# Prompts' keys as four more columns of each head's score product, in a two-branch cross-attention kernel

## The chip, the cores and the metric

The kernel runs on one core of a Trainium2 chip. Its time is the device time in microseconds of one execution, as the median of several runs. All data are 32-bit floats.

## What is computed

There are eight batches of 112 queries with 320 channels (20 heads of 16), and 375 context rows of 512 values each, of which the first 371 are text tokens and the last four are prompts. Cut to what matters, the reference is:

```python
q = heads(hidden_states @ W_q)
k_t, v_t = heads(text_ehs @ W_k), heads(text_ehs @ W_v)
probs_t = softmax(q @ k_t.T * attn_scale)
text_out = probs_t @ v_t
k_ip, v_ip = heads(ip_ehs @ W_k_ip), heads(ip_ehs @ W_v_ip)
attn_scores = q @ k_ip.T * attn_scale              # the prompts' logits: 112 x 4 a head
sem = l2norm(probs_t @ text_ehs) @ l2norm(ip_ehs).T
probs_ip = softmax(attn_scores + 0.5 * sem) * spatial_mask
out = (text_out + probs_ip @ v_ip) @ W_out + b_out + hidden_states
```

The change concerns how `attn_scores`, the prompts' logits, come about.

## The kernel before, in words

**Groups.** The 20 heads of a batch form five groups of four (`groups`, g = 0 to 4). A head takes 32 partitions of TensorE's rows, so the four heads of a group can run side by side. A loop runs over `steps`, all 35 pairs (batch b, group g) of the first seven batches; the last batch has a loop of its own with more work put on ACT and POOL.

**One step.** `multiplied(b, g)` (L618) makes twelve rounds of four products (L631, one for each head) of the transposed probabilities with a matrix of values and of context products, into four PSUM banks. In its rounds j = 0 and j = 6 stand the scores of the group two steps ahead (`LEAD`), heads 2 and 3 and then heads 0 and 1. `scores` (L575) is one product of 112 queries with 371 text keys (L584), out of `qm`, which holds the projected and scaled queries with the other head of a pair of heads masked out, and `kT`, the keys. `probabilities` (L593) follows: DVE takes the negated maximum (L597), ACT the Exp into `p` (L601), and SP starts a DMA of `p` to `xg` (L604). For the pair at j = 0 this follows at once; for the pair at j = 6 it comes after the step's copies of sums (`value_sums`, L644 on ACT). `transposed` (L608) is DVE's transposition of the next group's `xg` at j = 2 (L612), and `reduced` (L673) makes DVE's four sums over the products (L677), which free the four banks for the next step. `placed` (L549) lets POOL write the next group's values into `u` (L553).

**Between steps.** `between(b, g)` (L871) puts pieces of other work after each step: the next batch's context products (`gram`, L411), values (L480), keys (L447 and, for the last third, transpositions L438), the next queries (`project_queries`, L279), the transposed context (L353), and pieces of `finish` for the batch before (L693). At g = 3 of each batch up to the seventh stands `prompt_logits(b)` (L557), between two pieces of the keys, and for the last batch it stands in the last loop after g = 0.

**The prompts' logits.** `prompt_projections` (L241) projects all 32 prompts at once into `kip` (channels by prompts) and multiplies it with a mask of heads into `kipb`, which has for each prompt a column for every head of the third, zero outside the head's channels. `prompt_logits` then makes three products (L564) of the queries `qT` with those columns, into one bank, and ACT copies 112x80 logits into `ipl` (L571). For this alone `project_queries` copies each product of the queries to `qT` on ACT (L315), behind DVE's masked copies of the same bank to `qm` (L312). `finish` reads `ipl` at L746.

**Order and banks.** The orders of TensorE, SP, DVE and, after the start, ACT are those written in the code; POOL's is a scheduler's until the last loop. There are eight PSUM banks in three rotations: four `ps_qd` (products L631), two `ps_sc` (scores, and with `spare` some of ps_c, ps_x and ps_a), two `ps_mm` (all else, `bank`). A bank's next user waits for all who read its last content.

Of the kernel before, what the change touches and what calls it, by code (L numbers as in the profile page):

```python
# [14 lines left out]
NIP = 4  # L15
# [5 lines left out]
def kernel(  # L21
# [170 lines left out]

    ipT = const.tile([P, NE, N], F32, tag="ipT", name="ipT")
    ipnT = const.tile([P, NE, N], F32, tag="ipnT", name="ipnT")
    kipb = const.tile([P, NC, B, HC, NIP], F32, tag="kipb", name="kipb")
    vipd = dram.tile([N, C], F32, tag="vipd", name="vipd", bufs=1)

    vipx = dram.tile([2, H, NIP, C], F32, tag="vipx", name="vipx", bufs=1)
# [42 lines left out]
    def prompt_projections():  # L241

        spread(nc.gpsimd, wkip_sb)
        for i in range(NC):
            ps = bank(f"ps_kip{i}")
            for e in range(NE):
                nc.tensor.matmul(
                    ps[:, :N],
                    wkip_sb[:, e, i * P : (i + 1) * P],
                    ipT[:, e, :],  # L250
                    start=(e == 0),
                    stop=(e == NE - 1),
                )
            kip = work.tile([P, N], F32, tag="kip", name=f"kip_{i}")
            nc.scalar.copy(kip, ps[:, :N])
            nc.vector.tensor_tensor(
                kipb[:, i],
                kip.rearrange("p (b n) -> p b n", n=NIP).unsqueeze(2).to_broadcast([P, B, HC, NIP]),
                hmask.unsqueeze(1).unsqueeze(3).to_broadcast([P, B, HC, NIP]),
                ALU.mult,  # L260
            )
            yield
        ps = bank("ps_vip")
        for e in range(NE):
            nc.tensor.matmul(
                ps[:N, :C], ipT[:, e, :], wvip_sb[:, e, :], start=(e == 0), stop=(e == NE - 1)
            )
        vip = work.tile([N, C], F32, tag="vip", name="vip", bufs=1)
        nc.scalar.copy(vip, ps[:N, :C])
        yield  # L270

        nc.sync.dma_start(vipd, vip)
        yield
# [5 lines left out]
    def project_queries(bs):  # L279
        n = len(bs)  # L280
        xT = work.tile([P, NC, 2 * S], F32, tag="xT", name=f"xT_{bs[0]}", bufs=1)
        qT = work.tile([P, NC, 2 * S], F32, tag="qT", name=f"qT_{bs[0]}", bufs=2)
        qm = work.tile([P, NC, 2, 2 * S], F32, tag="qm", name=f"qm_{bs[0]}", bufs=2)
        for j, b in enumerate(bs):
            queries[b] = (qT, qm, j)
        nc.gpsimd.memset(xT[REST:, FULL, :], 0.0)
        for i in range(NC):
            cn = min(P, C - i * P)
            if bs[0] == 0:

                ps = ps_qd.tile([P, 512], F32, tag="qd", name=f"ps_x_0_{i}")
            else:
                ps = bank(f"ps_x_{bs[0]}_{i}", spare=bs[0] > 1 and i > 0)
            for j, b in enumerate(bs):
                nc.tensor.transpose(
                    ps[:cn, j * S : (j + 1) * S], x_sb[:, b, i * P : i * P + cn], ident[:S, :S]
                )
            nc.scalar.copy(xT[:cn, i, : n * S], ps[:cn, : n * S])
            yield
        for i in range(NC):  # L300
            ps = bank(f"ps_q_{bs[0]}_{i}")
            for j in range(NC):
                nc.tensor.matmul(  # L303
                    ps[:, : n * S],
                    wq_sb[:, j, i * P : (i + 1) * P],
                    xT[:, j, : n * S],
                    start=(j == 0),
                    stop=(j == NC - 1),
                )

            for r in range(2 if i < FULL else 1):
                nc.vector.tensor_scalar_mul(  # L312
                    qm[:, i, r, : n * S], ps[:, : n * S], emask[:, r : r + 1]
                )
            nc.scalar.copy(qT[:, i, : n * S], ps[:, : n * S])  # L315
            yield


# [6 lines left out]
    def begin(b):  # L325
        s = st[b] = dict(ct=loaded.pop(b))
        s["ctxT"] = work.tile([P, NE, TP], F32, tag="ctxT", name=f"ctxT_{b}")
        nc.gpsimd.memset(s["ctxT"][:, :, T:], 0.0)
        s["kT"] = work.tile([P, NC, TT], F32, tag="kT", name=f"kT_{b}")
        s["vext"] = work.tile([P, NT, C + REST], F32, tag="vext", name=f"vext_{b}", bufs=1)  # L330
        s["k3"] = k3
        s["vd"] = dram.tile([TP, C], F32, tag="vd", name=f"vd_{b}")
        s["u"] = work.tile([P, UCOL], F32, tag="u", name=f"u_{b}")
        s["vr"] = work.tile([P, BLK, NG, D], F32, tag="vr", name=f"vr_{b}")
        s["ipl"] = work.tile([S, H, NIP], F32, tag="ipl", name=f"ipl_{b}")
        s["ss"] = work.tile([S, H], F32, tag="ss", name=f"ss_{b}")
        s["pvs"] = work.tile([S, H, VW], F32, tag="pvs", name=f"pvs_{b}")
        s["vip"] = work.tile([S, NIP, H, D], F32, tag="vipb", name=f"vip_{b}")
# [90 lines left out]

    def keys(b):  # L430
        s = st[b]
        for i in range(NC):
            ps = bank(f"ps_k_{b}_{i}")
            if 0 < b < B - 1 and i == FULL:

                for c in range(NT):
                    rows = min(P, TT - c * P)
                    nc.tensor.transpose(  # L438
                        ps[:, c * P : c * P + rows],
                        s["k3"][:rows, c].rearrange("p a r d -> p (a r d)"),  # L440
                        ident[:rows, :rows],
                    )
                nc.scalar.copy(s["kT"][:, i, :], ps[:, :TT])
                yield
                return
            for e in range(NE):
                nc.tensor.matmul(  # L447
                    ps[:, :TT],
                    wk_sb[:, e, i * P : (i + 1) * P],
                    s["ctxT"][:, e, :TT],  # L450
                    start=(e == 0),
                    stop=(e == NE - 1),
                )
            nc.scalar.copy(s["kT"][:, i, :], ps[:, :TT])  # L454
            yield

    def last_keys(b, ps):

        s = st[b]
        for e in range(NE):  # L460
            if e == NE // 2:
                yield
            nc.tensor.matmul(  # L463
                ps[:, :TT],
                wk_sb[:, e, FULL * P :],
                s["ctxT"][:, e, :TT],
                start=(e == 0),
                stop=(e == NE - 1),
            )
        nc.scalar.copy(s["kT"][:, FULL, :], ps[:, :TT])  # L470
        yield

    def values(b):
# [81 lines left out]
            )  # L555

    def prompt_logits(b):  # L557
        s = st[b]
        qT, _, j = queries[b]
        ps = bank(f"ps_ip_{b}")  # L560
        for i in range(NC):
            heads = slice(0, HC, 1) if i < FULL else slice(0, HC, 2)
            hn = min(HC, H - i * HC)
            nc.tensor.matmul(  # L564
                ps[:S, i * HC * NIP : (i * HC + hn) * NIP],
                qT[:, i, j * S : (j + 1) * S],
                kipb[:, i, b, heads, :],
                start=True,
                stop=True,
            )  # L570
        nc.scalar.copy(s["ipl"], ps[:S, :HN].rearrange("p (h n) -> p h n", n=NIP))  # L571
        yield


    def scores(b, g, a, early=False, ps=None):  # L575
        s = st[b]
        _, qm, j = queries[b]
        i, r = g // 2, g % 2
        if early and (g + a // 2) % 2:

            ps = ps_qd.tile([P, 512], F32, tag="qd", name=f"ps_s_{b}_{g}_{a}")
        elif ps is None:
            ps = ps_sc.tile([P, 512], F32, tag="sc", name=f"ps_s_{b}_{g}_{a}")
        nc.tensor.matmul(  # L584
            ps[:S, :TT],
            qm[a * RG : (a + 1) * RG, i, r, j * S : (j + 1) * S],
            s["kT"][a * RG : (a + 1) * RG, i, :],
            start=True,
            stop=True,
        )  # L590
        s["sc", g, a] = ps

    def probabilities(b, g, a):  # L593
# [5 lines left out]
            s["p", g] = work.tile([S, GROUP, TT], F32, tag="p", name=f"p_{b}_{g}", bufs=3)  # L599
        p = s["p", g][:, a, :]  # L600
        nc.scalar.activation(p, ps[:S, :TT], AF.Exp, bias=nmx)  # L601

        xg = x_ring[(b * NG + g) % NX]
        nc.sync.dma_start(  # L604
# [259 lines left out]
    def run(key, make, pieces=1):  # L864

        if key not in gens:
            gens[key] = make()
        for _ in range(pieces):
            next(gens[key], None)

    def between(b, g):  # L871
# [26 lines left out]
        if g == 3:  # L898
            if new:
                run(("k", nb), None, 1)  # L900
            for bs in first if b > 0 else ():
                run(("q", bs[0]), lambda: project_queries(bs), 3)
            run(("t", b), lambda: prompt_logits(b))
            if nb < B - 1:
                run(("k", nb), None, 1)
            if b > 0 and new:
# [131 lines left out]
    for g in range(NG):  # L1038
# [30 lines left out]
        if g == 0:  # L1069
            own_channels(bd)  # L1070
            with_bias(b)
            drain(prompt_logits(b))
            run(("f", b - 2), None)
        if g == 1:
            prompt_values(b)
# [77 lines left out]
```

## Time and profile before

| what | value |
|---|---|
| median of 3 runs (lowest, highest) | 450.31 us (450.1, 450.73) |
| the profiled execution: its own time | 450.23 us |
| its span, from the first to the last instruction | 448.5 us |
| mean granted TensorE clock | 0.998 |
| L584 scores, matmul records | 320, 470 ns median |
| L564 prompts' logits, matmul records | 48, 262 ns median |
| L601 Exp | 160, 570 ns median |
| L571 copies to `ipl` | 8, 226 ns median |
| L315 copies to `qT` | 15, 346 ns median |

A line of the profile names an engine (PE for TensorE's matmuls, PEld for its weight loads, DVE for VectorE, ACT for ScalarE, POOL for GpSimd, SP for the engine that issues the DMAs), the line of the kernel, the operation, and what it writes and reads. A 32-bit product shows as two records. Matmul records overlap: they begin when the product begins to stream, so that the distance between two starts is what one costs the stream.

### The profile page before, as it was taken

What the parts mean: (1) busy time and instruction counts of PE and PEld (TensorE: products, weight loads), DVE (VectorE), ACT (ScalarE), POOL (GpSimd) and SP (SyncE); (2) the same over time, 40 slices, a digit from 0 to 9 for tenths busy, and PEclk for the clock granted to TensorE, in tenths of its full rate; (3) what the DMA queues carried; (4) which work ended last, traced back from release to release, by engine and by line L of the source; (5) the groups of instructions that cost most, each with busy time, mean ns of one, the idle gap of its engine ahead of it and who ended that gap; (6) DMA issues with size and microseconds to landing.
All of it is one profiled execution on the core that took longest, in us unless ns stands there. A gap on an engine that the chain in (4) does not pass through costs nothing.

```text
span 448.5 us, 12974 instructions
## 1 busy us (share of the span) xinstructions
PE 435.1 (97%) x5137; PEld 336.2 (75%) x5137; DVE 308.2 (69%) x649; ACT 194.1 (43%) x543; POOL 110.0 (25%) x263
## 2 busy tenths in 40 slices
PE   8998999999999999999999999999999999999885
PEld 8756767887778777788777786788777887787682
DVE  4047366786687767686687866776687867878784
ACT  2254233345335353343434453343534353346782
POOL 4302200012050211511142120512123111527430
PEclk9999999999999999999999999999999999999999
DMA  8669964544645565545646366455656437453500
GB/s 243 183 164 252 203 143 140 141 142 143 169 122 130 144 172 163 137 118 142 163 127 158 113 177 162 126 136 143 163 163 144 134 88 190 127 141 103 144 2 26
DMA packets 52158, 64.83 MB, mean 145 GB/s; under 512 B 18370, under 2 KB 44146, under 8 KB 52098
## 3 DMA queue, kind: packets, MB, share of 16 engines
q1 hardware_dynamic: 51658, 63.45, 53.7%
q8 instruction: 40, 0.66, 0.7%
q10 hardware_dynamic: 440, 0.56, 0.4%
q14 instruction: 20, 0.16, 0.1%
HBM read 19.30 MB, written 5.32 MB: 55 GB/s over the span
## 4 chain that ended last, share of the span: by engine, by line
PE 88%; DVE 3%; ACT 3%; DMA 3%; issue 1%; POOL 1%; SPq 1%; DVEq 0%; ACTq 0%
PE ps_qd L631 41%; PE ps_v L480 14%; PE ps_k L447 9%; PE ps_g L411 8%; PE ps_s L584 4%; PE ps_q L303 3%; PE ps_c L353 2%; PE ps_o L848 2%; DMA xg<-p 1%; ACT p L601 1%; PE ps_g L383 1%; DVE junk L677 1%; PE ps_ip L564 1%; DVE xgT L612 1%; PE ps_k L463 1%
## 5 line engine op out<-in xcount | busy, mean ns | idle before, releaser
L631 PE MATMUL ps_qd<-u,xgT 32*112 32x104 f32 (+11 forms) x3840 | 216.6, 352 | 3.6 <-POOL u L553 1.3
L631 PEld LDWEIGHTS ps_qd<-u,xgT 32*112 32x112 f32 x3840 | 182.5, 172 | 38.5 <-issue 9.8
L597 DVE TENSOR_REDUCE nmx<-ps_s 112x1 f32<-112x371 f32 x160 | 77.5, 529 | 73.3 <-PE ps_s L584 73.3
L612 DVE STREAM_TRANSPOSE xgT<-xg 128x1536 f32<-128x1536 f32 x40 | 118.9, 2973 | 8.7 <-DMA xg<-p 7.7
L601 ACT ACTIVATE p<-ps_s,nmx 112x371 f32<-112x371 f32 x160 | 82.4, 572 | 64.5 <-DVE nmx L597 46.7
L677 DVE CUSTOM_DVE_ANT_0 junk<-ps_qd,p 112x371 f32<-112x371 f32 x148 | 80.2, 542 | 15.6
L553 POOL COPY u<-vr 128x64 f32<-128x64 f32 x120 | 26.0, 238 | 169.8 <-PE ps_qd L631 112.5
L584 PE MATMUL ps_s<-kT,qm 32*112 32x371 f32 x320 | 63.5, 476 | 0.6 <-ACT p L601 0.4
L480 PE MATMUL ps_v<-wv_sb,ctxT 128*128 128x384 f32 (+1 forms) x192 | 63.5, 480 | 0.0
L480 PEld LDWEIGHTS ps_v<-wv_sb,ctxT 128*128 128x128 f32 x192 | 35.2, 190 | 19.7
L447 PE MATMUL ps_k<-ctxT,wk_sb 128*128 128x371 f32 x136 | 45.9, 482 | 0.0
L644 ACT COPY pvs<-ps_qd 112x21 f32<-112x21 f32 x150 | 16.1, 189 | 65.7 <-PE ps_qd L631 64.8
L411 PE MATMUL ps_g<-ctxT 128*128 128x375 f32 (+2 forms) x168 | 37.4, 379 | 0.0
L447 PEld LDWEIGHTS ps_k<-ctxT,wk_sb 128*128 128x128 f32 x136 | 25.1, 190 | 15.3 <-issue 0.5
L411 PEld LDWEIGHTS ps_g<-ctxT 128*128 128x128 f32 x168 | 28.1, 190 | 8.4
L584 PEld LDWEIGHTS ps_s<-kT,qm 32*112 32x112 f32 x320 | 25.5, 170 | 6.3 <-ACT kT L454 2.0
L312 DVE TENSOR_SCALAR qm<-ps_q,emask 128x224 f32<-128x224 f32 (+1 forms) x25 | 9.2, 400 | 24.5 <-PE ps_q L303 24.5
L487 ACT COPY vext<-ps_v 128x384 f32<-128x384 f32 (+1 forms) x24 | 11.2, 466 | 25.7 <-PE ps_v L480 25.2
L454 ACT COPY kT<-ps_k 128x371 f32<-128x371 f32 x17 | 8.0, 469 | 26.5 <-PE ps_k L447 26.5
L399 ACT ACTIVATE ug<-ps_g 128x375 f32<-128x375 f32 (+2 forms) x24 | 9.0, 377 | 23.5 <-PE ps_g L411 20.5
L817 POOL TENSOR_TENSOR wv<-vip,w 112x1280 f32<-112x1280 f32 x6 | 14.8, 2462 | 14.6 <-DVE w L761 14.6
L400 POOL TENSOR_TENSOR ug<-ug,half 128x128 f32<-128x128 f32 (+1 forms) x24 | 10.7, 450 | 29.9 <-ACT ug L399 29.9
(129 smaller groups left out, 336.1 us busy)
## 6 DMA issues: line engine op xcount, KB each, us to landing
xg<-p SPq DMA_DIRECT2D x160, 162.3 KB
u<-ug SPq DMA_DIRECT2D x128, 99.0 KB
ct<-in_ctx_dram SPq DMA_DIRECT2D x16, 256.0 KB
vip<-vipd SPq DMA_DIRECT2D x7, 560.0 KB
vr<-vd SPq DMA_DIRECT2D x32, 120.0 KB
vd<-vext SPq DMA_DIRECT2D x7, 320.0 KB
ct<-in_ctx_dram SPq DMA_DIRECT2D x8, 224.0 KB
vd<-vext SPq DMA_DIRECT2D x7, 160.0 KB
```

Source lines behind the costliest of these rows:

```text
L411: nc.tensor.matmul(ps[:, : T - t0], ctxT[:, e, t0 : t0 + P], ctxT[:, e, t0:T], start=(e == 0), stop=(e == NE - 1),)
L447: nc.tensor.matmul(ps[:, :TT], wk_sb[:, e, i * P : (i + 1) * P], s["ctxT"][:, e, :TT], start=(e == 0), stop=(e == NE - 1),)
L480: nc.tensor.matmul(ps[:, :w], ctxT[:, e, c * P : (c + 1) * P], wv_sb[:, e, :w], start=(e == 0), stop=(e == NE - 1),)
L553: nc.gpsimd.tensor_copy(region(b, c)[:, :, UV - c * P :], s["vr"][:, c * QN : (c + 1) * QN, g, :])
L584: nc.tensor.matmul(ps[:S, :TT], qm[a * RG : (a + 1) * RG, i, r, j * S : (j + 1) * S], s["kT"][a * RG : (a + 1) * RG, i, :], start=True, st ...
L597: nc.vector.tensor_reduce(nmx, ps[:S, :TT], AX.X, ALU.max, negate=True)
L601: nc.scalar.activation(p, ps[:S, :TT], AF.Exp, bias=nmx)
L612: nc.vector.transpose(xT.rearrange("p j (k q) -> p q j k", q=QN), xg.rearrange("p q (j k) -> p q j k", k=RG),)
L631: nc.tensor.matmul(banks[a][:S, j * RG : UW], xT[a * RG : (a + 1) * RG, j, :S], region(b, c)[a * RG : (a + 1) * RG, q, q * RG :], start=(j ...
L644: nc.scalar.copy(s["pvs"][:, h, :], ps[:S, TT:UW])
L677: nc.vector.tensor_tensor_reduce(out=junk, in0=ps[:S, :TT], in1=s["p", g][:, a, :], scale=1.0, scalar=0.0, op0=ALU.mult, op1=ALU.add, accu ...
L817: eng.tensor_tensor(wv, s["vip"][:, :, part], w.rearrange("p h n -> p n h").unsqueeze(3).to_broadcast([S, NIP, n, D]), ALU.mult,)
```

## The change

From the second batch on, `kT` has four more columns, written by POOL from `kip`, and each score product takes 375 columns in place of 371. Behind each Exp ACT copies the head's four logits from the score's bank to `ipl`. `prompt_logits` stays for the first batch alone; `qT` and `kipb` shrink to that batch.

```diff
-    kipb = const.tile([P, NC, B, HC, NIP], F32, tag="kipb", name="kipb")
+    kip = const.tile([P, NC, N], F32, tag="kip", name="kip")
+    kipb = const.tile([P, NC, HC, NIP], F32, tag="kipb", name="kipb")
...
-            kip = work.tile([P, N], F32, tag="kip", name=f"kip_{i}")
-            nc.scalar.copy(kip, ps[:, :N])
+            nc.scalar.copy(kip[:, i, :], ps[:, :N])
             nc.vector.tensor_tensor(
                 kipb[:, i],
-                kip.rearrange("p (b n) -> p b n", n=NIP).unsqueeze(2).to_broadcast([P, B, HC, NIP]),
-                hmask.unsqueeze(1).unsqueeze(3).to_broadcast([P, B, HC, NIP]),
+                kip[:, i, :NIP].unsqueeze(1).to_broadcast([P, HC, NIP]),
+                hmask.unsqueeze(2).to_broadcast([P, HC, NIP]),
                 ALU.mult,
             )
...
-            nc.scalar.copy(qT[:, i, : n * S], ps[:, : n * S])
+            if qT is not None:
+                nc.scalar.copy(qT[:, i, :], ps[:, :S])
...
-        s["kT"] = work.tile([P, NC, TT], F32, tag="kT", name=f"kT_{b}")
+        s["kT"] = work.tile([P, NC, T], F32, tag="kT", name=f"kT_{b}")
...
     def keys(b):
         s = st[b]
+        if b > 0:
+            nc.gpsimd.tensor_copy(s["kT"][:, :, TT:], kip[:, :, b * NIP : (b + 1) * NIP])
...
+        w = T if b > 0 else TT
         nc.tensor.matmul(
-            ps[:S, :TT],
+            ps[:S, :w],
             qm[a * RG : (a + 1) * RG, i, r, j * S : (j + 1) * S],
-            s["kT"][a * RG : (a + 1) * RG, i, :],
+            s["kT"][a * RG : (a + 1) * RG, i, :w],
...
         nc.scalar.activation(p, ps[:S, :TT], AF.Exp, bias=nmx)
+        if b > 0:
+            nc.scalar.copy(s["ipl"][:, groups[g][a], :], ps[:S, TT:T])
...
-            run(("t", b), lambda: prompt_logits(b))
+            if b == 0:
+                run(("t", b), lambda: prompt_logits(b))
...
-            drain(prompt_logits(b))
```

More of the change, by code (lines that the diff above doesn't have):

```diff
@@ L281, in project_queries @@
         xT = work.tile([P, NC, 2 * S], F32, tag="xT", name=f"xT_{bs[0]}", bufs=1)
-        qT = work.tile([P, NC, 2 * S], F32, tag="qT", name=f"qT_{bs[0]}", bufs=2)
         qm = work.tile([P, NC, 2, 2 * S], F32, tag="qm", name=f"qm_{bs[0]}", bufs=2)
+        qT = const.tile([P, NC, S], F32, tag="qT", name="qT") if bs[0] == 0 else None
         for j, b in enumerate(bs):
@@ L442, in keys @@
                     )
-                nc.scalar.copy(s["kT"][:, i, :], ps[:, :TT])
+                nc.scalar.copy(s["kT"][:, i, :TT], ps[:, :TT])
                 yield
@@ L453, in keys @@
                 )
-            nc.scalar.copy(s["kT"][:, i, :], ps[:, :TT])
+            nc.scalar.copy(s["kT"][:, i, :TT], ps[:, :TT])
             yield
@@ L469, in last_keys @@
             )
-        nc.scalar.copy(s["kT"][:, FULL, :], ps[:, :TT])
+        nc.scalar.copy(s["kT"][:, FULL, :TT], ps[:, :TT])
         yield
@@ L558, in prompt_logits @@
         s = st[b]
-        qT, _, j = queries[b]
+        qT = queries[b][0]
         ps = bank(f"ps_ip_{b}")
@@ L565, in prompt_logits @@
                 ps[:S, i * HC * NIP : (i * HC + hn) * NIP],
-                qT[:, i, j * S : (j + 1) * S],
-                kipb[:, i, b, heads, :],
+                qT[:, i, :],
+                kipb[:, i, heads, :],
                 start=True,
```

## The prediction

> **What bounds the kernel now.** I read the page's busy shares first, then the busy time in three stretches, then the chain that ended last, and last the timelines around the two places that the change touches. The times of single instructions below that the lines don't show are the trace's own start and end times.
>
> The page's first part says that TensorE is busy nearly all the time. The stretches 34 to 84, 84 to 400 and 400 to 448.5 us say where it isn't.
>
> ```profile
> PE 435.1 (97%) x5137; PEld 336.2 (75%) x5137; DVE 308.2 (69%) x649; ACT 194.1 (43%) x543; POOL 110.0 (25%) x263
> ```
>
> ```profile
> 84.00:400.00 316.00, 314.87 (x3865) 244.08 (x3864) 231.80 (x486) 134.69 (x377) 74.00 (x163) 1.00 0.55 145
> 400.00:448.50 48.50, 40.07 (x568) 31.63 (x566) 34.33 (x81) 30.19 (x90) 18.73 (x31) 0.98 0.25 70
> ```
>
> The columns after the window's length are busy PE, PEld, DVE, ACT and POOL. From 84 to 400 us TensorE lacks 1.1 us of being full, at a granted clock of 1.00. What is taken out of TensorE's stream there comes off the end, if no other engine is closer behind than the time taken out. ACT has half of that stretch free. Only the last 48 us have gaps (8.4 us).
>
> The chain says the same by line: the prompts' logits (L564) are a thing of about 1%.
>
> ```profile
> PE 88%; DVE 3%; ACT 3%; DMA 3%; issue 1%; POOL 1%; SPq 1%; DVEq 0%; ACTq 0%
> ```
>
> **Removed: the logits' products.** Eight sets of three products run before, seven go (the first batch keeps its own). This is the set of batch 2, in the timeline:
>
> ```profile
> 186.19 0.67 PE L564 MATMUL ps_ip<-kipb,qT 128*112 128x32 f32 x6
> ...
> 186.39 0.47 ACT L454 COPY kT<-ps_k 128x371 f32<-128x371 f32 x1 [1.27 <-PE ps_k L447]
> ...
> 187.01 0.51 PE L438 MATMUL ps_k<-ident,k 128*128 128x128 f32 x3
> ...
> 187.35 0.45 PE L835 MATMUL ps_a<-ident,attn 112*128 112x112 f32 x3
> ...
> 187.64 0.56 PE L303 MATMUL ps_q<-xT,wq_sb 128*128 128x224 f32 x2
> ```
>
> Ends overlap, so a step's price is the distance of starts. The set took 0.82 us here (186.19 to 187.01), of which the last 0.2 was not its own: L438 waited for the bank that ACT's copy of the keys (ended 186.86) gives back. I take the seven one by one, with the banks as they are dealt out after the change: the set took one of two rotating banks, so everything behind it moves to the other.
>
> - Batches 2 and 4: L438 gets the free bank and can start at 186.2; then L835, and L303 would be ready at 186.2 + 0.63 = 186.8. It now gets the bank that L438 waited for, free at about 187.0. So L303 starts at 187.0 instead of 187.64: 0.63 gained, 0.2 turned into a wait. Two times: 1.26.
> - Batches 1, 3 and 5: the set itself waited for that copy (135.38, ACT's end 135.33) and L438 followed at 135.99. L438 now does the waiting: 0.61 each, 1.83.
> - Batch 6: the set took 0.52 (391.79 to 392.31). But the transposition for the next batch's first group (L612, 396.10) already waits 0.13 for its DMA, and DVE's sums behind it end at 401.01; TensorE starts that group at 401.21 and its fourth head at 401.30. DVE and the DMA do not come 0.5 earlier. I take 0.2.
> - Batch 7: the set (406.61) is followed by L463 at 407.25, whose bank ACT gives back at 407.19. L463 waits for that anyway: 0.
>
> Sum: 1.26 + 1.83 + 0.2 = 3.3 us. It reaches the end only if DVE stays ahead: the fourth head of a group needs the bank of DVE's last sum, and at g = 4, where the savings come, that had slack of 1.6, 2.3, 1.7, 2.3 and 0.70 us in batches 1 to 5. All exceed 0.63; batch 5 is left with 0.09, and I give 0.1 back there.
>
> The Trainium skill ("TensorE: Matmul & The Clock Gate", Back-to-back issue gap) prices a matmul of up to 64 columns at some 25 ns apart, and 128 columns with their weights at 81 ns. The set is six records of 16 or 32 columns; by the rule they cost 0.15 to 0.5 us, by the row 0.1 each, 0.6. By the lower figure the seven are worth about 0.9 us. The trace is of this f32 form, so 0.6 stands.
>
> **Removed: twelve copies of the queries** (L315, 0.25 to 0.35 us on ACT, each standing behind DVE's L312). In the trace nothing on TensorE waits for them. Worth 0; ACT loses 4 us and seven logits' copies of 0.23.
>
> **Added: four columns to 140 products.** Two records of a product start 321 ns apart with another product beside them (192.467 and 192.788), and 224 columns start 191 ns apart at L303: 0.83 ns a column and record. Four columns are 3.3 ns, times two records; the two heads of a pair run side by side, so a group pays 2 x 6.7 = 13 ns, and 35 groups 0.5 us at most; where the other heads' products fill in, half. I take 0.25.
>
> **Added: 140 copies on ACT, and where they stand.** The place that matters is the second pair of scores in a group, which takes the two banks that the first pair gives back. Batch 3, group 1:
>
> ```profile
> 190.47 0.99 DVE L597 TENSOR_REDUCE nmx<-ps_s 112x1 f32<-112x371 f32 x2 [0.66 <-PE ps_s L584]
> ...
> 191.10 1.03 ACT L601 ACTIVATE p<-ps_s,nmx 112x371 f32<-112x371 f32 x2 [0.91 <-DMA vr<-vd]
> ...
> 192.38 0.27 PEld L584 LDWEIGHTS ps_s<-kT,qm 32*112 32x112 f32 x4
> 192.47 0.49 PE L584 MATMUL ps_s<-kT,qm 32*112 32x371 f32 x2
> ```
>
> The second Exp ends at 192.131 and the second head's weights go in at 192.391. The 0.26 us between repeats within 0.01 in nearly every group after the first batch. Of it ACT's signal takes 0.04 to 0.05 (kT's end at 135.325 to L564's weights at 135.376), so 0.21 is left. Now each Exp is followed by a copy of 112x4 before the bank is free. The nearest row:
>
> ```profile
> L644 ACT COPY pvs<-ps_qd x150: 166/183/232, 41.8 to 437.5; 112x21 f32<-112x21 f32 x150
> ```
>
> Such copies start 0.07 apart (194.339, .413, .481, .549), and ACT issues the next instruction 0.45 to 0.47 after an Exp's start, before the Exp ends (195.166 Exp, 195.618 ctxT's copy). So the second Exp comes 0.07 later, and its copy ends 0.46 + 0.17 - 0.56 = 0.07 after it. Together 0.14, under 0.21: no stall. What ends last there stays TensorE's own stream. If the copies could not overlap, each would add 0.17 to 0.18 twice, 0.36: 0.15 over, in 32 groups, 4.8 us.
>
> The Trainium skill speaks against the change here: "ScalarE: Activation LUTs", Rules for kernel authors, budgets about 0.3 us for every ACTIVATE before its elements. By it the bank would come 0.6 late, 0.4 past the slack, 12 us in 32 groups. The row of L644 is the same instruction over PSUM and shows 0.07 between starts; I follow the row.
>
> Elsewhere the copies cost nothing: the first pair of the next group comes over 3 us after its banks; ps_c, ps_x and ps_a, which share them, come 0.3 us or more behind the late release. The DMA of p (L604) is issued 0.93 apart by SP, so a second head that is 0.07 late hides behind the first. In the last batch ACT carries four Exps in the chain (419.63 to 421.58), and three copies delay the last by 0.2; but SP issues their DMAs at 420.23, 421.16, 422.09 and 423.00, so the last has 1.4 us of cover, without which it costs 0.2.
>
> **Added: waits on TensorE's sequencer.** The copy sits between Exp and the next product in that bank, and in the program as built the second pair's products each wait for TensorE's own earlier product as well as for ACT; a second wait is an instruction of its own. There are 80 more of them in all, 64 in these 32 pairs. The products of the group queue behind. The trace has such instructions: 51 ns each, and where TensorE stood still before them (429.43) the heads behind came 0.125 apart. In a running stream of L631 one was dealt with at 193.848, 12 records and 0.39 us ahead of its product. At the pair, 12 records are 0.54 us (191.928 to 192.467); two waits take 0.25. Bounds: 0, and 0.25 in 32 groups, 8 us. A gain is excluded: they replace nothing. I take 0, by the stream's row.
>
> **Small edits.** Seven copies of 128x12 on POOL into the keys' columns: POOL is 25% busy, and the nearest (ctxT, 128x16) takes 0.20; they come before the keys are used, some 3 us or more. Three products on DVE for kipb shrink from 256 to 32 columns in the first batch, where DVE has 6 us of slack. Both 0. SP's order is unchanged.
>
> **Sum.** The profiled execution took 450.23 us, the span 448.5 and 1.7 around it; the median of the runs is 450.31. 450.23 - 3.3 + 0.1 + 0.25 = 447.3.
>
> **The rivals.** Measurement tells about 0.2% (0.9 us) from no change.
> - Savings swallowed: DVE's sums or the DMA of p are as close as TensorE at g = 4, and the new wait moves behind them. For it: slack of 0.70 in batch 5, the DMA wait of 0.13 at 396.10. Against it: more than 1.6 in four of five. If two thirds go: 449.4. Chance 0.12.
> - The bank late by 0.1 us, if a copy behind an Exp costs more than one behind a copy: 32 x 0.1 = 3.2, 450.5. Against it is the ctxT copy above. Chance 0.10.
> - Slower: TensorE's queue is not ahead at the pair, since 64 short waits follow matmuls of 0.17 us for four heads. If one of two waits is bare, 0.125 x 32 = 4.0: 451.3. It makes the kernel slower from 0.094 us a group (3.0 / 32). For it: the 0.125 at 429.43; against it the lead of 0.39. Chance 0.14.
> - The forecast, 446.4 to 448.4: chance 0.64.
>
> The range from 446.4 to 450.5 holds the forecast, the first rival and half of the second. Faster takes the forecast and half of the first, 0.71; same the rest of the first and most of the second, 0.13; slower 0.16.
>
> **What would show it.** Right: L438 waits for the keys' copy in batches 1, 3 and 5, L303 in 2 and 4, by some 0.2; the second pair's weights still come about 2.83 us after the first pair's products; copies of ipl end 0.07 after their Exp; the fourth head in batch 5, g = 4 starts with the others. Wrong: a pair of scores whose two heads start 0.1 apart (waits), weights that start 0.04 after a copy of ipl (bank), or a first group of products held by DVE.

## The result, and the profile after

The changed kernel takes 448.51 us (median of 7 runs, 447.55 to 449.33) beside 450.73 us of the kernel before on the same chip (7 runs, 450.1 to 451.76). The ratio is 0.9953 with a 95% interval of 0.994 to 0.9966: faster by 1.5 to 2.7 us, clearly more than the 0.2% that can be told from no change, and less than the forecast 3.0. The profiled execution took 449.23 us, with a span of 447.5.

The page of the changed kernel has the busy shares and, further down, the shares of the chain that ended last:

```profile
PE 435.1 (97%) x5095; PEld 336.3 (75%) x5095; DVE 308.9 (69%) x649; ACT 196.5 (44%) x664; POOL 111.1 (25%) x270
...
PE 86%; DVE 4%; ACT 4%; DMA 3%; issue 1%; POOL 1%; SPq 1%; DVEq 0%; POOLq 0%; ACTq 0%
```

TensorE has 42 records less and ACT 121 more instructions, as the diff says. The chain still lies on TensorE. DVE and ACT each have one per cent more of it. In the two stretches the columns are, after the length, busy PE, PEld, DVE, ACT and POOL, then the granted clock:

```profile
84.00:400.00 316.00, 314.97 (x3847) 244.09 (x3849) 234.53 (x491) 138.28 (x487) 75.96 (x170) 1.00 0.54 145
400.00:447.50 47.50, 39.66 (x553) 31.48 (x545) 33.25 (x75) 29.35 (x96) 17.99 (x31) 0.96 0.24 71
```

From 84 to 400 us TensorE is as full as before. So the gain is what was taken out of its stream, less what waits came into it. The last stretch had a granted clock of 0.96 where it was 0.98 before; that matters below.

**Where the time went.** I laid the starts of the 40 groups of products (the first of the twelve rounds of each group) of both traces beside each other. In the first batch the changed kernel is 0.33 us late, and constantly so, since TensorE went over to its full pace later: its matmuls stand 0.21 us apart until 7.2 us and 0.11 from there, in the kernel before until 6.1 us. From there:

| place | forecast | measured, before to after |
|---|---|---|
| gaps behind g = 3 of batches 2 and 4 | -0.63 each | -0.64, -0.64 |
| the same of batches 1, 3 and 5 | -0.61 each | -0.35, -0.35, -0.46 |
| the same of batch 6 | -0.2 | -0.55 |
| group (5, 4) | +0.1 | +0.61 |
| columns, all other groups and small gaps | +0.25 | +0.33, of it 0.011 in nearly every group from (0, 4) on |
| from group (0, 0) to (7, 1) | -2.95 | -2.05 |
| from (7, 1) to the end | 0 | +0.74 |

With the 0.33 of the start, -2.05 + 0.74 + 0.33 = -0.98, the 1.0 by which the two spans differ. Four of these rows are not what the prediction said; the runs below take them one by one.

The even batches came as foreseen. The timeline of the changed kernel in batch 2:

```profile
186.29 0.48 PE L444 MATMUL ps_k<-ident,k 128*128 128x128 f32 x3
...
186.49 0.47 ACT L460 COPY kT<-ps_k 128x371 f32<-128x371 f32 x1 [1.12 <-PE ps_k L453]
...
186.61 0.45 PE L845 MATMUL ps_a<-ident,attn 112*128 112x112 f32 x3
...
187.01 1.05 PEld L305 LDWEIGHTS ps_q<-xT,wq_sb 128*128 128x128 f32 x6 [0.16 <-ACT kT L460]
```

The keys' transpositions (L444) stand where the logits stood, the transposed outputs (L845) follow, and the queries (L305) wait 0.16 us for ACT's copy of the keys. In the odd batches another wait comes in. Batch 1 of the kernel before, ACT's copy of the keys and TensorE behind it:

```profile
134.86 0.47 ACT L454 COPY kT<-ps_k 128x371 f32<-128x371 f32 x1 [1.25 <-PE ps_k L447]
...
135.38 0.76 PE L564 MATMUL ps_ip<-kipb,qT 128*112 128x32 f32 x6
135.99 0.52 PE L438 MATMUL ps_k<-ident,k 128*128 128x128 f32 x3
136.35 0.45 PE L835 MATMUL ps_a<-ident,attn 112*128 112x112 f32 x3
```

And of the changed kernel:

```profile
135.06 0.74 PE L297 MATMUL ps_x<-ident,x_sb 112*128 112x112 f32 x6
...
135.26 0.47 ACT L460 COPY kT<-ps_k 128x371 f32<-128x371 f32 x1 [1.13 <-PE ps_k L453]
...
135.63 0.82 ACT L300 COPY xT<-ps_x 128x224 f32<-128x224 f32 x3
...
135.88 0.51 PE L444 MATMUL ps_k<-ident,k 128*128 128x128 f32 x3
...
136.34 0.30 PEld L845 LDWEIGHTS ps_a<-ident,attn 112*128 112x128 f32 x3 [0.19 <-issue]
136.37 0.48 PE L845 MATMUL ps_a<-ident,attn 112*128 112x112 f32 x3
```

L444 waits for the copy of the keys (ended 135.73), as foreseen, but starts 0.15 after it, since the wait is an instruction of its own on TensorE (51 ns, at 135.77). In the kernel before, the logits' first product carried that wait itself and started 0.05 after the copy (135.33). And L845 has 0.50 from L444 where it had 0.36, so TensorE stood still a second time. Its bank is one that ACT's second copy of `xT` gives back, which ended at 136.23.

### The profile page after: what moved, and what is told of

The parts are those of the page before. It is cut to its first block, busy times and chain, and to the rows that moved or that the text cites. A ratio compares the mean times of both kernels' runs of the same rounds, so it can differ in the third digit from the quotient of the medians.

```text
span 447.5 us, 13078 instructions
## 1 busy us (share of the span) xinstructions
PE 435.1 (97%) x5095; PEld 336.3 (75%) x5095; DVE 308.9 (69%) x649; ACT 196.5 (44%) x664; POOL 111.1 (25%) x270
## 4 chain that ended last, share of the span: by engine, by line
PE 86%; DVE 4%; ACT 4%; DMA 3%; issue 1%; POOL 1%; SPq 1%; DVEq 0%; POOLq 0%; ACTq 0%
PE ps_qd L641 39%; PE ps_v L486 13%; PE ps_g L415 8%; PE ps_k L453 8%; PE ps_s L592 4%; PE ps_q L305 3%; PE ps_o L858 3%; DMA xg<-p 3%; PE ps_c L357 2%; DVE xgT L622 2%; ACT p L609 2%; PE ps_g L387 1%; DVE junk L687 1%; PE ps_w L374 1%; PE ps_k L469 1%
## 5 line engine op out<-in xcount | busy, mean ns | idle before, releaser
L641 PEld LDWEIGHTS ps_qd<-u,xgT 32*112 32x112 f32 x3840 | 185.8, 172 | 36.7 <-issue 10.3
L609 ACT ACTIVATE p<-ps_s,nmx 112x371 f32<-112x371 f32 x160 | 86.9, 582 | 80.7 <-DVE nmx L605 58.0
L592 PE MATMUL ps_s<-kT,qm 32*112 32x375 f32 (+1 forms) x320 | 64.8, 481 | 0.4 <-ACT p L609 0.4
L611 ACT COPY ipl<-ps_s 112x4 f32<-112x4 f32 x140 | 23.5, 168 | 0.0
```

The source lines that it names most:

```text
L592: nc.tensor.matmul(ps[:S, :w], qm[a * RG : (a + 1) * RG, i, r, j * S : (j + 1) * S], s["kT"][a * RG : (a + 1) * RG, i, :w], start=True, st ...
L611: nc.scalar.copy(s["ipl"][:, groups[g][a], :], ps[:S, TT:T])
L641: nc.tensor.matmul(banks[a][:S, j * RG : UW], xT[a * RG : (a + 1) * RG, j, :S], region(b, c)[a * RG : (a + 1) * RG, q, q * RG :], start=(j ...
```

## The experiments

All ratios below are to the kernel before on the same chip; the changed kernel's own is 0.9953. Of each edit the lines that matter are shown. Single executions move by about 1 us with the clock that is granted in the first and last microseconds, so I read most verdicts from the starts of the groups, which repeat within some 0.01 us in the groups that no late DMA disturbs; these are called steady.

**The removed part alone.** No columns, no copies, no added waits: the prompts' logits are left out from the second batch on and stand as zeros.

```diff
+        if b > 0:
+            nc.gpsimd.memset(s["ipl"], 0.0)
...
-        if b > 0:
-            nc.gpsimd.tensor_copy(s["kT"][:, :, TT:], kip[:, :, b * NIP : (b + 1) * NIP])
...
-        w = T if b > 0 else TT
+        w = TT
...
-        if b > 0:
-            nc.scalar.copy(s["ipl"][:, groups[g][a], :], ps[:S, TT:T])
```

> The removed part alone: no added columns, no copies to ipl, no added waits; the prompts' logits of batches 2 to 8 are left out and stand as zeros. Theory (the copies and the waits are hidden; the columns cost the 0.011 us that each of 32 groups shows; in the last batch the four copies cost 0.24): 0.35 + 0.24, about 0.6 us below the changed kernel, each group from the second batch on shorter by 0.01, and the gaps in the odd batches as large as in the changed kernel. Rival (the copies' later release of the banks, or the 64 waits, cost time in every group): 32 groups shorter by 0.05 or more, 1.6 us or more below the changed kernel.

Measured 448.26 us, ratio 0.9951 (0.9937 to 0.9964). The steady groups are 0.000 longer than before, where the changed kernel's are 0.011 longer. The gaps of batches 1 to 4 are -0.353, -0.639, -0.350 and -0.639, the changed kernel's to 0.004. So everything that the change added costs 0.011 us a group in the body, and the shortfall of the odd batches belongs to the removal. The whole, though, is not 0.6 below the changed kernel: with 0.9951 beside 0.9953 the two can't be told apart. The groups (5, 4), (6, 0) and (7, 0) are 0.14, 0.31 and 0.72 longer than before, each time behind a transposition that waited for a late DMA of p, of which more below.

**The copies on DVE, without the 64 waits.**

```diff
+        if b > 0:
+            nc.vector.tensor_copy(s["ipl"][:, groups[g][a], :], ps[:S, TT:T])
         nc.scalar.activation(p, ps[:S, :TT], AF.Exp, bias=nmx)
-        if b > 0:
-            nc.scalar.copy(s["ipl"][:, groups[g][a], :], ps[:S, TT:T])
```

> The copies of the four logits made by DVE, ahead of the Exp, which also takes away the 64 separate waits on TensorE and gives the banks back with the Exp as before. Theory (waits and banks are hidden): the groups as long as in the changed kernel within 0.02 us; in the last batch the last Exp 0.1 to 0.2 us earlier, since ACT carries no copies; so 0 to 0.3 us below the changed kernel. Rival (TensorE's waits or the bank cost): 0.05 or more in 32 groups, 1.6 us or more below the changed kernel.

Measured 449.65 us, ratio 0.9978 (0.9966 to 0.999). The steady groups are again 0.010 to 0.012 longer than before, with the 64 separate waits gone: these waits cost nothing there. The expected time was missed by about 1 us. In the body three groups are clearly longer than before: (5, 4) by 0.75 (0.61 in the changed kernel), (6, 3) by 0.27 and (7, 0) by 0.78. The first and the last are held by the DMA of p. In (6, 3) it is DVE, which here carries the copies: its last sum ends 0.35 later against the start of the group than in the changed kernel. Another 0.27 lies around the start of batch 1.

**Each copy three times.**

```diff
-            nc.scalar.copy(s["ipl"][:, groups[g][a], :], ps[:S, TT:T])
+            for _ in range(3):
+                nc.scalar.copy(s["ipl"][:, groups[g][a], :], ps[:S, TT:T])
```

> Each copy of the four logits is made three times, all on ACT. At 0.07 us between starts the second bank of a pair comes 4 x 0.07 = 0.28 us later. Theory (the bank has 0.10 to 0.15 us to spare): the second pair's products start 0.13 to 0.18 us late in 32 groups, 4 to 6 us above the changed kernel, less where TensorE takes the other heads' products meanwhile. Rival (the release is not near the edge, and ACT's order hides it): within 0.3 us of the changed kernel. Rival (the bank is already late in the changed kernel): the full 0.28 in 32 groups, 9 us above it.

Measured 470.95 us, ratio 1.0466 (1.0437 to 1.0495), far above every number expected. The edit was not what I took it for: since the three copies have one target, each waits for the one before, and they start 0.19 to 0.21 apart instead of 0.07. This kernel at the scores of batch 3, group 1:

```profile
198.00 0.57 ACT L609 ACTIVATE p<-ps_s,nmx 112x371 f32<-112x371 f32 x1 [2.84 <-DVE nmx L605]
...
198.46 0.54 ACT L612 COPY ipl<-ps_s 112x4 f32<-112x4 f32 x3
198.90 0.58 ACT L609 ACTIVATE p<-ps_s,nmx 112x371 f32<-112x371 f32 x1
...
199.33 0.27 PEld L592 LDWEIGHTS ps_s<-kT,qm 32*112 32x112 f32 x2
199.37 0.55 ACT L612 COPY ipl<-ps_s 112x4 f32<-112x4 f32 x3
...
199.97 0.17 PEld L592 LDWEIGHTS ps_s<-kT,qm 32*112 32x112 f32 x1
```

The second head's weights go in at 199.97, 0.05 behind the last copy (199.92), and no longer beside those of the first head at 199.33. With the delay known, the run still gives the number it was made for. From the start of its group to the end of the last copy it is 4.09 us (3.36 in the changed kernel), 0.73 more, and the group is 0.64 longer. So 0.09 us of spare were left at the bank in the changed kernel.

The changed kernel's own timeline at the same scores:

```profile
190.56 0.57 ACT L609 ACTIVATE p<-ps_s,nmx 112x371 f32<-112x371 f32 x1 [2.89 <-DVE nmx L605]
...
191.03 0.15 ACT L611 COPY ipl<-ps_s 112x4 f32<-112x4 f32 x1
191.07 0.58 ACT L609 ACTIVATE p<-ps_s,nmx 112x371 f32<-112x371 f32 x1
...
191.53 0.17 ACT L611 COPY ipl<-ps_s 112x4 f32<-112x4 f32 x1
191.85 0.27 PEld L592 LDWEIGHTS ps_s<-kT,qm 32*112 32x112 f32 x4
```

The copy starts before its Exp ends, and the next Exp 0.04 behind the copy's start. The release moves by 0.12 (3.24 to 3.36 from the group's start) and the weights stay at 3.50.

**The prompts' values one batch earlier.** Group (5, 4) was the largest single loss: DVE's transposition ahead of it waited 1.24 us for the DMA of p. In that batch a transfer through DRAM, `vipx` (L525), has its packets from 324.4 to 330.1 us.

```diff
-        if (b, g) == (B - 3, 1):
+        if (b, g) == (B - 4, 1):
```

> The changed kernel with the reordering of the prompts' values through DRAM (the transfer to vipx, 40 packets of 5120 bytes, one behind another) one batch earlier, in the fifth batch in place of the sixth. Theory (in the sixth batch's last group the DMA of p is late because these packets stand in its queue, which makes the fourth head 0.42 and the group 0.6 us late): that group is as long as those of the other odd batches, 0.4 to 0.6 us below the changed kernel; in the fifth batch nothing is late, since its DMA has 1.6 us of slack there. Rival (the DMA of p is late of itself in that group, since DVE and SP are there as late as the products): the group stays 0.6 longer, and the time within 0.2 us of the changed kernel.

> The kernel before with the prompts' values reordered one batch earlier, nothing else. Theory (there the DMA of p in the sixth batch's last group was late too, by 0.86 us of DVE's wait, but TensorE was later still by 0.70): that wait goes, and the groups stay as long as before, within 0.05 us each; the time within 0.3 us of before. Rival (moving that transfer is worth 0.6 us whatever the kernel): 0.4 us or more below before.

Measured 448.41 us, ratio 0.9948 (0.9934 to 0.9962), for the changed kernel, and 450.83 us, ratio 1.0002 (0.9983 to 1.002), for the kernel before with the same edit. Group (5, 4) is now 0.008 longer than before instead of 0.607, and in the kernel before its length doesn't change (+0.001), as expected: there the transposition waits 0.86, and DVE's last sum behind it still ends 0.29 ahead of TensorE. The wait moved with the transfer: the transposition for (4, 4) now waits 0.78 in the changed kernel, but DVE has more room there, and the group keeps its length. The transposition in the two changed kernels:

```profile
336.50 3.00 DVE L622 STREAM_TRANSPOSE xgT<-xg 128x1536 f32<-128x1536 f32 x1 [1.24 <-DMA xg<-p]
```

```profile
334.73 3.01 DVE L622 STREAM_TRANSPOSE xgT<-xg 128x1536 f32<-128x1536 f32 x1
```

My reason was half wrong: p's packets do not stand behind those of `vipx`. The view of waits of SP, 326 to 332 us of the changed kernel, says what does:

```profile
SPq L614 <- ACT ipl L611: 1.1, 1, 1.1
SPq L614 <- DMA vipx<-vipd: 0.8, 1, 0.8
```

SP did not issue the DMA of p before the `vipx` transfer had landed. In the program as built these DMAs share eight semaphores in turn (numbers 100 to 107 in the trace), and each waits for the one eight places ahead of it to have landed. L525 stands eight places ahead of the third p of group (5, 4). Measured from the start of the group, that p is issued at 8.71 before, 8.63 after, 8.06 in keep_qT and 8.69 in remove_only, and at 7.71 or 7.72 in the four where `vipx` goes a batch earlier. (In copies_dve it is 8.96, by an issue of SP that took 2.13.) What reaches TensorE varies, since it hangs on how long the p itself takes then: 0.607 in the changed kernel, 0.144, 0.748 and 0.010 in remove_only, copies_dve and keep_qT, with the transposition waiting 1.24, 0.71, 1.16 and 0.20. Over the runs the edit gained little: a ratio of 0.9948 beside 0.9953, within the intervals.

How the group comes to lose 0.61 can be read from DVE's last sum and the fourth head, whose bank that sum gives back. First the kernel before, then the changed one:

```profile
343.27 0.55 DVE L677 CUSTOM_DVE_ANT_0 junk<-ps_qd,p 112x371 f32<-112x371 f32 x1
...
344.09 0.93 PE L631 MATMUL ps_qd<-u,xgT 32*112 32x392 f32 x8
```

```profile
342.27 0.54 DVE L687 CUSTOM_DVE_ANT_0 junk<-ps_qd,p 112x371 f32<-112x371 f32 x1
...
342.88 0.17 PEld L641 LDWEIGHTS ps_qd<-u,xgT 32*112 32x112 f32 x1 [0.35 <-DVE ss L687]
```

Before, the sum ends at 343.82 and the fourth head's first record starts at 344.11, 0.02 behind the first head's: 0.29 of room. In the changed kernel TensorE comes to the group 0.44 earlier, counted from group (5, 2), and the sum ends 0.40 later, since the transposition comes 0.40 later. The head starts 0.06 behind the sum. 0.44 + 0.40 - 0.29 + 0.06 = 0.61. The same count gives 0.15 for remove_only and 0.75 for copies_dve, as measured.

**The queries' copies put back on ACT**, into a buffer that nobody reads.

```diff
-            if qT is not None:
+            if bs[0] == 0:
                 nc.scalar.copy(qT[:, i, :], ps[:, :S])
+            else:
+                nc.scalar.copy(qk[:, i, : n * S], ps[:, : n * S])
```

> The changed kernel with the twelve copies of the queries put back on ACT (into a buffer that nobody reads). Theory (they were covered): every group as in the changed kernel, and the gaps behind the fourth groups within 0.1 us; the time within 0.3 us of it. Rival (part of the gain came from ACT being free at the fourth groups, where keys, transposed queries and outputs wait for ACT's copies): the gaps in the even batches lose 0.3 us of their 0.64, 0.6 to 1.5 us above the changed kernel.

Measured 448.22 us, ratio 0.9947 (0.993 to 0.9965). The gaps of batches 1 to 6 are -0.352, -0.639, -0.349, -0.639, -0.525 and -0.554. Nothing of the gain came from the twelve copies.

**Another bank for the transposed outputs in the odd batches**, on top of the edit on `vipx`.

```diff
-        ps = bank(f"ps_a_{b}_{h0}", spare=not late)
+        ps = bank(f"ps_a_{b}_{h0}", spare=not late and b % 2 == 1)
```

> The changed kernel with the prompts' values reordered one batch earlier, and the transposition of attn (ps_a) in the batches 1, 3 and 5 of the loop put into the bank that ACT's first copy of the transposed context rows of queries gives back, in place of the one of the second copy, 0.25 us later. Theory (in these batches 0.14 of the missing 0.25 is the wait for that second copy): the gaps behind the fourth groups of batches 1, 3 and 5 widen their gain from 0.35 to 0.45-0.49, 0.3 to 0.4 us in all below the version with the prompts' values alone moved. Rival (the group behind is held by something else, DVE's sums or the keys' own wait): the gaps stay at 0.35. Rival (the banks dealt out afterwards fall worse): the gain comes back as a wait in the next gap.

Measured 447.8 us, ratio 0.9939 (0.9921 to 0.9957). The gaps of batches 1, 3 and 5 are -0.528, -0.525 and -0.526. In the first two that is 0.18 more than without it. Batch 5 has -0.53 without it too, in after_vip, keep_qT and remove_only; the -0.46 of the changed kernel has a wait of 0.06 at L297, for a bank that ACT's copy to `ipl` gives back, which those three don't have. In batch 1 of this kernel the outputs follow at once:

```profile
136.03 0.51 PE L444 MATMUL ps_k<-ident,k 128*128 128x128 f32 x3
...
136.38 0.45 PE L845 MATMUL ps_a<-ident,attn 112*128 112x112 f32 x3
```

0.35 behind L444, as before the change. The remaining 0.08 of the 0.61 is L444's own wait. In the same profile group (7, 0) was 0.46 longer than before, and the reason is SP again. The first line is from a_bank, the second from the changed kernel; both are the four transfers of `u` that stand ahead of the second pair's p:

```profile
386.32 3.16 SPq L429 DMA_DIRECT2D u<-ug  x4
```

```profile
387.18 2.73 SPq L429 DMA_DIRECT2D u<-ug  x4
```

Each of these issues takes 0.58 to 0.59; in a_bank one took 1.26, in the changed kernel 0.83. Somewhere in this stretch one took 1.66 in copies_dve and 1.05 in remove_only. So the DMA of p for group (7, 0) came late in three of these profiles, and each time TensorE lost 0.46 to 0.78.

**The last batch's logits the old way**, with the edit on `vipx`.

```diff
-        w = T if b > 0 else TT
+        w = T if 0 < b < B - 1 else TT
...
-        if b > 0:
+        if 0 < b < B - 1:
             nc.scalar.copy(s["ipl"][:, groups[g][a], :], ps[:S, TT:T])
...
+            drain(prompt_logits(b))
```

> The changed kernel with the prompts' values reordered one batch earlier, and with the last batch's prompts' logits made by the old three products and one copy, so that its score products have 371 columns and ACT copies nothing behind its Exps. Theory (the four copies of the last group stand in ACT's chain from the last Exps to the end and cost 0.24; the old three products cost nothing there, since the keys' last third waits for a bank anyway): the last Exp and all of ACT behind it 0.2 to 0.3 us earlier, as seen from the last batch's second group, than with the prompts' values alone moved; the groups of the last batch without the 0.2 that its fourth shows. Rival (SP's issues cover the last Exp, as the prediction has it): no change behind the last Exp, or 0.5 us later by the old products.

Measured 448.01 us, ratio 0.9948 (0.9931 to 0.9965): the same ratio as with the edit on `vipx` alone. ACT's timeline shows the part that was in doubt. The changed kernel, last group:

```profile
417.92 0.57 ACT L609 ACTIVATE p<-ps_s,nmx 112x371 f32<-112x371 f32 x1 [1.84 <-POOL shared L676]
418.39 0.15 ACT L611 COPY ipl<-ps_s 112x4 f32<-112x4 f32 x1
418.43 0.58 ACT L609 ACTIVATE p<-ps_s,nmx 112x371 f32<-112x371 f32 x1
...
419.90 0.21 ACT L611 COPY ipl<-ps_s 112x4 f32<-112x4 f32 x1
420.13 1.28 ACT L746 ACT_TABLE_LOAD   x1
```

and with the old way in the last batch:

```profile
416.58 1.95 ACT L610 ACTIVATE p<-ps_s,nmx 112x371 f32<-112x371 f32 x4 [1.84 <-POOL shared L677]
418.55 1.28 ACT L747 ACT_TABLE_LOAD   x1
```

From the first Exp to the table load it is 2.21 us with the copies and 1.97 without, as before the change: 0.24 on ACT's own chain. The fourth group, 0.200 longer in the changed kernel, is as long as before (0.000). How much the end of the run gained by it this profile doesn't show, since its last DMA of p happened to land 4.15 us after its issue, beside 3.42 in the changed kernel.

The `a_bank` and `last_old_vip` edits were not run together.

## Why the prediction was right in direction and too large

**Even batches: right.** 0.63 was forecast, 0.64 measured in every profile, with the wait of the queries for the keys' copy where it was said to be. The rule of the Trainium skill on small matmuls ("TensorE: Matmul & The Clock Gate", Back-to-back issue gap) would have given, as an estimate, 0.15 to 0.5 a set; the row of the trace held.

**Odd batches: the mechanism right, the size wrong.** The step that failed is "L438 now does the waiting: 0.61 each". It followed one bank and took the step behind it (L835, now L845) as free. That one takes the other kind of bank, which ACT's copies of `xT` were only just giving back: 0.18 (a_bank). And the wait, which the logits' first product had carried in its own weight load, became a separate instruction in the place where nothing was queued ahead: 0.08.

**Batch 6: 0.2 forecast, 0.55 gained.** The step that failed read the transposition's 0.13 of waiting (396.10) as "DVE and the DMA do not come 0.5 earlier". They did. In the profile of before, the DMA of p for that group was late through SP:

```profile
386.65 2.52 SPq L604 DMA_DIRECT2D xg<-p  x2
```

Two issues that take 0.8 each lasted 2.52 together, one of them 1.60. In before_vip the same two lasted 2.16 and the transposition waited for nothing: what stood in the one profile like a limit was a late issue. Where SP isn't held up so long the room is there, as the changed kernel, after_vip and keep_qT show; where it is, up to 0.78 is lost.

**Batch 5: 0.1 given back forecast, 0.61 in the profile.** The step that failed is the slack of 0.70. The place was rightly named, but the room was 0.29: the distance of 0.70 leads to the eighth record of the group (344.53), the fourth head's second, and not to its first (344.11). Counted so, the slacks at g = 4 of batches 1 to 4 are 1.2, 1.9, 1.2 and 1.8 in place of 1.6, 2.3, 1.7 and 2.3, still enough. In batch 5 the 0.61 that the forecast took off would have met 0.29, less the 0.06 of the signal: 0.4 to give back, not 0.1. In the changed kernel TensorE came 0.44 earlier, which alone gives 0.21; the other 0.40 is a later p. The sum left out why p was late there at all: SP waits for `vipx`, which before_vip shows to have been so, and hidden, before the change. In the changed kernel it also took 4.82 from p's last issue to the transposition and not 4.36; that is not explained. This is the forecast's first rival (savings swallowed by the DMA of p), in one of the batches.

**Columns, copies, banks and waits: right.** 0.011 a group against a bound of 0.013 (of the two distances that the prediction divides one gives 0.87 and the other 0.85 ns a column, not 0.83, which changes nothing); 0.12 of later release against 0.14; 0.09 spare against 0.07. ACT's fixed 0.3 us by the Trainium skill ("ScalarE: Activation LUTs", Rules for kernel authors) would, as an estimate, have made the release 0.6 late, and the row of the neighbouring copy was the better guide. The rivals of the late bank and of the bare waits fall: the steady groups are the same to 0.011 us with neither (remove_only), with the copies on DVE and no waits (copies_dve), and with both. TensorE has 80 more wait instructions in the changed kernel (196 beside 116), as counted beforehand. Bare waits do show in the last batch, where TensorE's queue is short: the heads of the fourth group start up to 0.25 apart, and it is 0.20 longer or more in every kernel that has the waits there and not in those without.

**The last batch: 0 forecast, about 0.2 lost.** The step that failed is "the last has 1.4 us of cover". It looked at what follows an Exp on SP and not at what follows it on ACT: the table load and the sharing of the last outputs come right behind the fourth copy, 0.24 later. Counted from the start of group (7, 1), the first and the last of ACT's six table loads start at 10.90 and 27.60 us in a_bank, at 10.66 and 27.36 in the kernel before: the 0.24 stays to the end. From the same start the run goes on for 37.69 and 37.71 us in a_bank and keep_qT, for 37.54, 37.48 and 37.48 in before, before_vip and remove_only: 0.15 to 0.23. In copies_dve the first load is early too (10.67), but the last four are 0.32 late and the end is at 37.77; why is not traced.

**The rest of the end is the clock.** The changed kernel itself took 38.28 from the same point, with the same last batch as a_bank. The stretches of 4 us that begin 30 us after that point, first of the changed kernel, then of a_bank:

```profile
439.23:443.23 4.00, 3.17 (x9) 1.73 (x9) 2.02 (x6) 0.60 (x2) 0.00 (x0) 0.68 0.11 36
```

```profile
438.73:442.73 4.00, 2.69 (x10) 1.33 (x9) 2.03 (x6) 0.60 (x2) 0.00 (x0) 1.00 0.11 36
```

The granted clock (the last column but two) was 0.68 in the one and 1.00 in the other, and TensorE was busy 0.48 longer. So the profiled execution (449.23) lies 1.9 us above the forecast 447.3: 0.9 in the body, about 0.2 by the last batch's copies, about 0.6 by this fall of the clock and 0.3 at the start. How the 1.2 of the median split is not measured, since it is another execution. Of the ten profiles two have the fall, for 3.4 us each: the changed kernel's, from 440.65 us, and after_vip's. In the other eight the clock stays at 1.00 until TensorE's last product is done. What decides it is not shown: in the 3.41 us before the fall TensorE was busy for 2.66, as in a like stretch of the kernel before (439.57 to 442.98), behind which the clock stayed. Over the runs of the changed kernel the mean clock lies between 0.993 (449.33 us) and 1.000 (447.58 us).

## What to carry to other kernels

When a step is taken out of an engine's stream, follow every resource of each step behind it, its kind of bank, the copy that frees it, and the form of its wait, until one of them was not later than before; one step was not far enough here. A slack is counted to the record that really needs the bank, here the fourth and not the eighth. A wait that stands in one profile once should be checked against the same place in another execution and, if it is a DMA, back to the issue: a stretched issue differs from one execution to the next (1.60 and 1.24 us at the same place), a semaphore shared with a slow transfer eight places ahead is there each time and can be moved. A cheap instruction added to an engine is free only as long as something else lies behind it on that same engine that isn't due; in the last batch the same four copies cost 0.24 us.

## What the runs showed that was not expected

- Single DMA issues of SP that take 0.58 or 0.80 us took 1.05 to 2.13 now and then (L604 before: 801 ns at least, 827 median, 1682 at most). They are not scattered at random. In the ten profiles, from 30 us on, 58 issues of `u` and p took over 0.2 us longer than usual, and 53 of these stand across a packet of 16 KB on the queue that the page calls "q8 instruction"; of the 2628 others 255 do. There are 40 such packets in each profile, about one a group, and in before and before_vip one begins at 387.5 and 387.4, at the stretched p of group (7, 0). That the packet holds SP up is likely by this, and no run tried it.
- An ACT copy that has to wait for the copy right before it starts 0.19 to 0.21 us behind that one, one that needn't 0.07.
- The `vipx` transfer, 40 packets of 5120 bytes, took 7.1 to 7.8 us from its issue until SP went on. Where a transposition waited for p (from batch 1 on), it started 3.2 to 4.8 us after the issue of the fourth head's p, 112 x 371 values.
